# Last layer's first three groups score three quarters of the keys early; the feature bias by small products; the mixing's layernorm as a step of its own

## The chip, the cores and the metric

The kernel runs on 1 core of one Trainium2 chip. The time is the device time of one launch in microseconds (us). Five engines work side by side, each through its own queue in order: TensorE (PE in the profile; its weight loads are the row PEld), VectorE (DVE), ScalarE (ACT), GpSimd (POOL) and SyncE (SP), which here only issues DMAs.

## The reference

2048 tokens of 128 features go through four layers, each an attention and a feed-forward with a layernorm ahead of each and a residual add behind it.

```python
x = x + _L0_attn_ref(_layernorm(x), ...)   # softmax attention, 16 heads of 64
x = x + _L0_ffn_ref(_layernorm(x), ...)    # 8 experts, top one, with capacity
x = x + _L1_attn_ref(_layernorm(x), ...)   # causal attention, 16 heads of 64
x = x + _L1_ffn_ref(_layernorm(x), ...)    # mixing with the token before
x = x + _L2_attn_ref(_layernorm(x), ...)   # kernel weights that fold to one product
x = x + _L2_ffn_ref(_layernorm(x), ...)    # ternary weights, 128 -> 512 -> 128
x = x + _L3_attn_ref(_layernorm(x), ...)   # region mask and a feature bias
x = x + _L3_ffn_ref(_layernorm(x), ...)    # binary weights, 128 -> 512 -> 128
```

The parts that the change touches are the mixing and the last attention:

```python
x_prev = jnp.concatenate([jnp.zeros((B, 1, C), x.dtype), x[:, :-1, :]], axis=1)
xr = mu_r * x + (1.0 - mu_r) * x_prev
xk = mu_k * x + (1.0 - mu_k) * x_prev
r = jax.nn.sigmoid(jnp.einsum('btc,dc->btd', xr, W_r))
k_act = jnp.square(jax.nn.relu(jnp.einsum('btc,dc->btd', xk, W_k)))
out = r * jnp.einsum('btc,dc->btd', k_act, W_v)
...
hmid = jax.nn.gelu(jnp.einsum('bnd,fdk->bfnk', x, ext_w1) + ext_b1[None, :, None, :], approximate=False)
feature_scores = jax.nn.sigmoid(jnp.einsum('bfnk,fk->bfn', hmid, ext_w2) + ...).transpose(0, 2, 1)
dots = jnp.einsum('bhid,bhjd->bhij', q, k) * scale
dots = jnp.where(mask[None, None, :, :], dots, neg)
bias = jnp.einsum('bnf,hf->bhn', feature_scores, fw)[..., None]
attn = jax.nn.softmax(dots + bias, axis=-1)
```

The bias is one number for each query and head.

## The kernel before

**Tiles and stages.** The residual stream `x` lies in SBUF as 16 tiles of 128 tokens by 128 features, and its normalised transpose `xT` beside it (L277 writes it). Four tiles are a quarter of the tokens. An attention layer (class `Attention`) goes through 8 pairs of heads; a pair (class `Pair`) makes keys `kT`, queries `qT` and values `v` by quarters (L390, L399, L411, L418). Each pair has 8 groups of 256 queries (class `Group`), and a group has 8 strips of 32 queries.

**A strip.** For each of the two heads, `score` multiplies 32 queries with all keys into one PSUM bank (L482): the keys are split in four, each a product of 32 rows in its own quarter of the partitions, so a strip is a tile of 128 x 512 scores. There are four banks, two strips. `scan` (L492) lets VectorE copy a bank to SBUF (`e`) and take the minimum of each row. When four strips are scanned, `spread_lowest` brings the minima of the four parts of a query together: a transpose (L544), a reduction on VectorE (L552), a copy on GpSimd (L560), a transpose back (L567), and the shift (L586, in the last layer L578, which adds the bias; there GpSimd has first taken the bias off the minima, L536). ScalarE then makes the exponentials in place (L594), VectorE transposes them in blocks of 32 (L611), TensorE multiplies them with the values (L626), and L645 to L699 divide by the sums, project and add to `x`. The tile `e` has six buffers, two for each group in the last layer.

**The passage to the last layer.** When the second attention layer is done with a span of tokens, the function `rest` takes that span through the mixing (L1070 to L1136), the folded third attention (L1087, L1145) and the ternary feed-forward (`feed_forward`, L955 to L988), with a layernorm (`normalise`, L241 to L277) ahead of each and one more for the last layer. The spans are tiles 0 to 3, 4 to 7, 8 to 11, 12 and 13, 14 and 15. A span's mixing needs the last token of the span before; L1091 saves its column in `edge`, because the next layernorm overwrites `xT`. `features` makes the bias for a quarter: three products and Gelus (L1194, L1199), a product and a Sigmoid (L1207, L1213), then four times a GpSimd copy that repeats the scores of 32 tokens four times (L1221), four products with the weights of the heads (L1228) and a VectorE copy of 64 columns into `bias` (L1234).

**What sets the order.** No order is written by hand. Every step is a `Step` with an engine, an estimated duration, a key and the steps and buffers that it needs. The key begins with a tick, a number handed out by `planner(tick)`; smaller goes first. The function `run` goes through the steps once, keeps a clock for each engine from the estimates, and issues the first step in key order that can start, or one that fits into the time until then. What comes out is a fixed order for each engine; on the chip each engine works through its own in that order and waits for semaphores. A change of an estimate or of a tick can so move instructions anywhere. Buffers come from rings (`Ring`, `Held`), and most rings hand them out in key order. The layers' ticks are set here:

```python
L1 = Attention("L1", L0.begin + 32 * HP, 0.125 * 0.125, causal=True)
L3 = Attention("L3", L1.begin + 32 * HP, 0.125, masked=True, bias=bias)
...
for t0, n in spans:
    rest(planner(L1.left(t0, n)), t0, n, L1.outputs(t0, n) + [bu_added[t0 // 4]], n < 4, made)
```

and a group's scoring needs the keys of all four quarters:

```python
needs = pair.k_made[0 : self.g // 2 + 1 if causal else 4] + [pair.q_made[self.g // 2]]
```

Of the kernel before, what the change touches and what calls it, by code (L numbers as in the profile page):

```python
# [13 lines left out]
ALU = mybir.AluOpType  # L14
# [44 lines left out]
def network(ctx: ExitStack, tc: tile.TileContext, a: dict, out: bass.AP):  # L59
# [18 lines left out]
    class Ring:  # L78


        def __init__(self, pool, name, shape, bufs, ordered=True):
            self.bufs, self.takers, self.held, self.ordered = bufs, [], [], ordered
            self.make = lambda: pool.tile(list(shape), F32, tag=name, name=name, bufs=bufs)
            rings.append(self)

    class Held:


        def __init__(self, ring):
            self.ring, self.users = ring, []  # L90
# [28 lines left out]
    def run():  # L119
# [18 lines left out]
        for _ in range(len(steps)):  # L138
# [18 lines left out]
            for h in s.takes:  # L157
                h.t = h.ring.make()
# [30 lines left out]
    LOW, SHIFT = Ring(small, "low", [P, 2, 4], 3), Ring(small, "shift", [P, 2, 4], 3)  # L189
    ALL_LOW, ALL_LOW4 = Ring(small, "all_low", [NS, Q], 2), Ring(small, "all_low4", [NS, 4, Q], 2)  # L190
# [43 lines left out]
    def normalise(add, t0, n, after, before=(), row=None, hurry=False):  # L234


        mv, xn, pt = Held(MEANS), Held(NORMED), Held(MISC)
# [57 lines left out]
    class Attention:  # L295
# [53 lines left out]
        def plan(self):  # L349
            for p in range(HP):  # L350
# [3 lines left out]
                for g, first, weigh in groups:  # L354
                    Group(pair, g, begin + first, late, begin + weigh)
# [10 lines left out]
    class Pair:  # L366
# [19 lines left out]
        def projected(self, add, c, to, which, s, takes):  # L386
            pp, b = Held(MISC), self.layer.biases[which]
# [18 lines left out]
        def valued(self, add, c):  # L406
            pv, v = Held(MISC), self.v[c]
# [13 lines left out]
    class Group:  # L421


        def __init__(self, pair, g, t0, late, t1):
# [3 lines left out]
            self.sums, self.o, self.oT = Held(SUMS), Held(SUMMED), Held(OUT)  # L428
            self.lows, self.shifts = [Held(LOW) for j in range(2)], [Held(SHIFT) for j in range(2)]
            scanned = [self.score(planner(t0 + k, SCORES), planner(t0 + k, LOWEST), k) for k in range(4)]  # L430
# [28 lines left out]
        def score(self, add, add_scan, k):  # L459
# [5 lines left out]
            def make(i, s):  # L465
                n, strip = self.width(i), NS * self.g + i
                own = bass.ts(strip, Q)
                for h in range(2):
                    half = bass.ds(DH * h, DH)
                    for c in range(4):  # L470
                        on = bass.ts(c, Q)
                        q = pair.qT[self.g // 2].t[half, bass.ts(strip % 16, Q)]
                        keys = blocks(pair.kT.t[half, 0 : 4 * n], c)
# [3 lines left out]
                        if masked and strip == 0:  # L477
                            terms.append((0, n, picks[half, 0:Q], blocks(regions[half, :], c)))
                        if masked and c == 0:
# [10 lines left out]
            def scan(i, h, s):  # L490
                n = self.width(i)
                nc.vector.tensor_scalar(  # L492
                    self.e(h)[:, i, 0:n], s.t[:, 0:n], 1.0, None, ALU.mult, ALU.min,
                    accum_out=self.lows[j].t[:, h, i % 4 : i % 4 + 1],
                )

            needs = pair.k_made[0 : self.g // 2 + 1 if causal else 4] + [pair.q_made[self.g // 2]]
# [911 lines left out]
```

## Time and profile before

| what | value |
|---|---|
| time, median of 3 runs | 3634.2 us (3632.11 to 3635.78) |
| time of the profiled execution | 3627.2 us |
| its span, first to last instruction | 3625.3 us |
| TensorE busy, matmuls | 3522.5 us (97%) |
| VectorE busy | 3333.3 us (92%) |
| ScalarE busy | 2611.1 us (72%) |
| GpSimd busy | 574.6 us (16%) |
| L492, scans, 3072 | 1658.7 us |
| L611, transposes of the exponentials, 768 | 1504.6 us |
| L594, exponentials, 3072 | 1969.3 us |

A busy TensorE is not TensorE at its peak, since matmuls overlap and their ends are modelled; an engine that is busy in one stage can be idle in another, so the shares of the whole span say little about any stage. The page shows the span in 40 equal slices, in tenths of busy time, with the TensorE clock that was granted:

```profile
PE   8999999999999999999999988899999999999998
DVE  8999999999999979888888874699999999999995
ACT  5677777777777667788888866477776766777775
PEclk9999999999999999999999998899999999999999
```

A slice is 90.6 us. The dip of VectorE in slices 24 and 25, from about 2170 to 2350 us, is the passage to the last layer.

### The profile page before, as it was taken

To read this page: it belongs to the slowest core of one execution; us is meant where nothing else is said; L and a number is where in the kernel's file an instruction comes from. 1 tells how busy PE (TensorE), PEld (TensorE's weight loads), DVE (VectorE), ACT (ScalarE), POOL (GpSimd) and SP (SyncE) were. 2 spreads that over 40 slices of the span, in tenths; PEclk is the share of its full clock that TensorE was granted. 3 is DMA by queue.
4 is the path that set the end of the run, shared out by engine and by line. 5 is a ranking of instruction groups with operands and counts; after the bars stand their busy time and mean duration, and the time that the engine had idled before them with its cause. 6 is when DMAs were issued, how large, how long until landed. Compare 5 with 4: busy or idle time off the path is not lost. (4 is left out here: it accounts for less than half of the span.)

```text
span 3625.3 us, 112352 instructions
## 1 busy us (share of the span) xinstructions
PE 3522.5 (97%) x46250; PEld 1798.6 (50%) x46250; DVE 3333.3 (92%) x8275; ACT 2611.1 (72%) x7940; POOL 574.6 (16%) x1172
## 2 busy tenths in 40 slices
PE   8999999999999999999999988899999999999998
PEld 3444444444444455655555645445444454444544
DVE  8999999999999979888888874699999999999995
ACT  5677777777777667788888866477776766777775
POOL 1111011101111242111111134111111111111112
PEclk9999999999999999999999998899999999999999
DMA  1000000000000000000000000000000000000000
GB/s 45 2 5 2 5 5 2 5 2 5 5 2 5 1 5 8 6 6 6 6 6 6 6 2 4 4 5 5 2 5 2 5 5 2 5 2 2 2 5 10
DMA packets 22938, 18.77 MB, mean 5 GB/s; under 512 B 3556, under 2 KB 21612, under 8 KB 22426
## 3 DMA queue, kind: packets, MB, share of 16 engines
q1 hardware_dynamic: 22362, 11.55, 1.1%
q8 instruction: 363, 5.95, 0.7%
q14 instruction: 149, 1.22, 0.1%
q0 software_dynamic: 64, 0.06, 0.0%
HBM read 10.60 MB, written 1.05 MB: 3 GB/s over the span
## 5 line engine op out<-in xcount | busy, mean ns | idle before, releaser
L594 ACT ACTIVATE e<-e,shift 128x512 f32<-128x512 f32 (+15 forms) x3072 | 1969.3, 644 | 182.0 <-DVE shift L578 174.9
L492 DVE TENSOR_SCALAR_CACHE_REDUCE e<-s 128x512 f32<-128x512 f32 (+15 forms) x3072 | 1658.7, 588 | 58.1 <-PE s L482 57.0
L482 PE MATMUL s<-kT,qT 64*32 64x512 f32 (+8 forms) x24576 | 1514.0, 534 | 25.5 <-DVE e L492 24.1
L611 DVE STREAM_TRANSPOSE e<-e 128x2048 f32<-128x2048 f32 (+10 forms) x768 | 1504.6, 1961 | 21.9 <-ACT e L594 20.7
L626 PE MATMUL o<-e,v 128*64 128x256 f32 (+1 forms) x10496 | 1302.4, 386 | 13.3 <-DVE e L611 11.9
L626 PEld LDWEIGHTS o<-e,v 128*64 128x64 f32 x10496 | 731.1, 137 | 587.6 <-issue 233.4
L482 PEld LDWEIGHTS s<-kT,qT 64*32 64x32 f32 x24576 | 429.1, 105 | 490.2 <-DVE e L492 239.0
L594 ACT ACTIVATION_READ_ACCUMULATOR e<-e,shift 128x1 f32 x3072 | 580.0, 189 | 0.0
L560 POOL COPY all_low<-all_low 8x128 f32<-8x128 f32 x384 | 108.0, 281 | 1953.3 <-DVE all_low L552 1953.3
L699 POOL TENSOR_TENSOR x<-x,part 128x256 f32<-128x256 f32 x384 | 280.7, 731 | 562.8 <-ACT part L681 547.4
L681 ACT ACTIVATE part<-t,r 128x128 f32<-128x128 f32 x768 | 218.8, 366 | 148.9 <-PE t L671 144.8
L686 ACT COPY oT<-o 128x256 f32<-128x256 f32 x192 | 70.7, 368 | 274.7 <-PE o L626 274.6
L492 DVE DVE_READ_ACCUMULATOR e<-s 128x1 f32 x3072 | 229.7, 75 | 0.0
L390 PE MATMUL t<-xT,w 128*128 128x512 f32 x384 | 204.2, 625 | 2.7 <-ACT xT L277 2.0
L482 PE MATMUL s<-beyond,eye 64*32 64x32 bf16 x2560 | 159.8, 177 | 0.0
L671 PEld LDWEIGHTS t<-w,oT 64*128 64x128 f32 x1536 | 103.9, 188 | 98.3 <-issue 67.2
L671 PE MATMUL t<-w,oT 64*128 64x128 f32 x1536 | 141.4, 299 | 2.8 <-ACT oT L686 1.5
L482 PEld LDWEIGHTS <-regions 64*32 64x32 bf16 x1024 | 74.4, 93 | 130.1 <-issue 105.3
L586 ACT COPY shift<-t 128x8 f32<-128x8 f32 x256 | 42.2, 165 | 131.0 <-PE t L567 131.0
L552 DVE TENSOR_REDUCE all_low<-t 8x32 f32<-8x128 f32 x384 | 100.7, 262 | 27.8 <-PE t L544 26.9
L482 PE MATMUL s<-picks,regions 64*32 64x8 bf16 x1024 | 122.1, 166 | 0.0
L567 PEld LDWEIGHTS t<-ident,all_low 8*128 8x128 f32 x384 | 51.2, 133 | 134.9 <-issue 75.9
(181 smaller groups left out, 1790.8 us busy)
## 6 DMA issues: line engine op xcount, KB each, us to landing
w<-in_L_wq SPq DMA_DIRECT2D x24, 64.0 KB, 1.9
w<-in_L_wk SPq DMA_DIRECT2D x24, 64.0 KB, 2.1
w<-in_L_wv SPq DMA_DIRECT2D x24, 64.0 KB, 2.0
w<-in_L_wo SPq DMA_DIRECT2D x24, 64.0 KB, 2.1
x<-in_x SPq DMA_DIRECT2D x4, 256.0 KB, 4.7
out_x<-x SPq DMA_DIRECT2D x3, 256.0 KB, 2.3
big<-in_L_wo SPq DMA_DIRECT2D x1, 512.0 KB
big<-in_moe_w SPq DMA_DIRECT2D x1, 512.0 KB
```

Source lines behind the costliest of these rows:

```text
L390: nc.tensor.matmul(pp.t, lhsT=self.w.t[:, which, :], rhs=xT[:, cols(4 * c, 4)], start=True, stop=True)
L482: nc.tensor.matmul(s[h].t[on, bass.ds(first, size)], lhsT=lhsT, rhs=rhs, start=m == 0, stop=m == len(terms) - 1,)
L492: nc.vector.tensor_scalar(self.e(h)[:, i, 0:n], s.t[:, 0:n], 1.0, None, ALU.mult, ALU.min, accum_out=self.lows[j].t[:, h, i % 4 : i % 4 + 1],)
L552: lambda: nc.vector.tensor_reduce(all_low.t, pm.t[0:NS, 0:P].rearrange("p (c q) -> p q c", q=Q), AX.X, ALU.min),
L560: lambda: nc.gpsimd.tensor_copy(all_low4.t, all_low.t.unsqueeze(1).to_broadcast([NS, 4, Q])),
L594: nc.scalar.activation(e, e, AF.Exp, bias=self.shifts[j].t[:, h, i % 4 : i % 4 + 1], scale=-1.0, accum_out=self.sums.t[:, h, i : i + 1],)
L611: nc.vector.transpose(e, e)
L626: nc.tensor.matmul(self.o.t[bass.ds(DH * h, DH), first(t) : NS, :], lhsT=self.pair.v[c].t[:, t % 4, bass.ds(DH * h, DH)], rhs=self.e(h)[:, ...
L671: nc.tensor.matmul(y[h].t[:, bass.ts(j, P)], lhsT=oT.t[half, bass.ts(j, P)], rhs=pair.w.t[half, 3, :], start=True, stop=True,)
L681: nc.scalar.mul(part.t[:, j, :], y[h].t[:, bass.ts(j, P)], r.t[:, j, h : h + 1])
L686: lambda: nc.scalar.copy(oT.t, self.o.t.rearrange("p i q -> p (i q)")),
L699: POOL, 0.74, lambda part=part: nc.gpsimd.tensor_tensor(xs, xs, part.t, ALU.add), [divided], uses=[part]
```

## The change

**Early scores.** In the last layer's first pair, groups 0 to 2 score in two parts. The first part is the keys of the first three quarters (384 of the 512 columns), with a tick 12 below the layer's begin, and needs only those keys; its minima go to a ring `first_low` of six buffers. The second part is the last quarter (128 columns). A VectorE minimum (128 x 8) joins the two before the rest of `spread_lowest`. The region mask's products are split along. All other groups score as before.

**Feature bias.** GpSimd's copies are gone. The scores of a quarter, as they are, are multiplied with the weights of the heads (4 products into 64 columns), ScalarE copies these, 16 products with columns of the identity put each strip's rows into the four parts of the partitions, and one VectorE copy of 256 columns writes `bias`.

**The mixing's layernorm.** It leaves `rest` and becomes `first_norm`, which is planned for all spans ahead of the rests of all spans, with the same ticks. `edge` has a column for each tile instead of two that take turns.

**Ticks and estimates.** The last layer begins 14 ticks later. The estimates for scoring and transposing are changed. Buffers get names of their own, which changes no instruction.

```diff
+                    early = begin - 12 + first if p == 0 and g < 3 and self.masked else None
+                    Group(pair, g, begin + first, late, begin + weigh, early)
...
-            scanned = [self.score(planner(t0 + k, SCORES), planner(t0 + k, LOWEST), k) for k in range(4)]
+            parts = [(t0, 0, 4, self.lows)]
+            if early is not None:
+                self.firsts = [Held(FIRST) for j in range(2)]
+                parts = [(early, 0, 3, self.firsts), (t0, 3, 4, self.lows)]
+            scanned = [[] for k in range(4)]
+            for tick, c0, c1, lows in parts:
+                for k in range(4):
+                    scanned[k] += self.score(planner(tick + k, SCORES), planner(tick + k, LOWEST), k, c0, c1, lows)
...
-            needs = pair.k_made[0 : self.g // 2 + 1 if causal else 4] + [pair.q_made[self.g // 2]]
+            needs = pair.k_made[c0 : self.g // 2 + 1 if causal else c1] + [pair.q_made[self.g // 2]]
...
-            us = max(0.25, 0.0019 * n) + (0.1 if causal else 0.07 if masked else 0.0)
+            us = max(0.25, 0.002 * n) + (0.14 if causal else 0.05 if masked else 0.0)
...
+            for some in self.firsts[j : j + 1]:
+                found = [
+                    add(
+                        DVE,
+                        0.1,
+                        lambda some=some: nc.vector.tensor_tensor(low.t, low.t, some.t, ALU.min),
+                        found,
+                        uses=[low, some],
+                    )
+                ]
...
-            return add(DVE, 0.06 + 0.00436 * self.width(4 * j), do, made, uses=self.rows)
+            return add(DVE, 0.05 + 0.0042 * self.width(4 * j), do, made, uses=self.rows)
...
+    def first_norm(add, t0, n, after, hurry):
+        done, _ = normalise(add, t0, n, after, L1.readers[t0 // 4], hurry=hurry)
+        last = t0 + n - 1
+        to, some = edge[:, last : last + 1], xT[:, bass.ds(PAD + P * (t0 + n) - 1, 1)]
+        kept[t0 + n] = add(DVE, 0.15, lambda: nc.vector.tensor_copy(to, some), [done])
+        return done
...
+        def weigh():
+            for i in range(4):
+                nc.tensor.matmul(
+                    pbias.t[:, bass.ts(i, H)], lhsT=fs.t[0:NF, bass.ts(i, P)], rhs=fwT, start=True, stop=True
+                )
+
+        def hand_out():
+            for q in range(4):
+                for i in range(4):
+                    nc.tensor.matmul(
+                        pall.t[bass.ts(q, Q), bass.ts(i, 4 * H)],
+                        lhsT=ident[:, bass.ts(i, Q)],
+                        rhs=some.t[:, 0 : 4 * H],
+                        start=True,
+                        stop=True,
+                    )
+
+        def copy():
+            to = bias[:, bass.ts(c, 16), :].rearrange("p (t i) h -> p i t h", i=4)
+            nc.vector.tensor_copy(to, pall.t[:, 0 : 16 * H].rearrange("p (i t h) -> p i t h", i=4, h=H))
...
-            made = add(POOL, 0.6, spread, [scored], takes=[some], uses=[fs])
-            add(PE, 0.8, weigh, [made, fwT_made], takes=[pbias], uses=[some])
-            L3.biased[c].append(add(DVE, 0.16, copy, uses=[pbias]))
+        add(PE, 0.6, weigh, [scored, fwT_made], takes=[pbias, some], uses=[fs])
+        made = add(ACT, 0.25, lambda: nc.scalar.copy(some.t[:, 0 : 4 * H], pbias.t[:, 0 : 4 * H]), uses=[pbias, some])
+        add(PE, 1.2, hand_out, [made], takes=[pall], uses=[some])
+        L3.biased[c].append(add(DVE, 0.4, copy, uses=[pall]))
...
-    L3 = Attention("L3", L1.begin + 32 * HP, 0.125, masked=True, bias=bias)
+    L3 = Attention("L3", L1.begin + 32 * HP + 14, 0.125, masked=True, bias=bias)
```

## The prediction, made before the changed kernel ran

> **What bounds the kernel now.** I read the busy time by stretches of the span first, then the chain of waits through the passage from the third layer into the last one, then VectorE's and TensorE's timelines there, then the groups of instructions by shape. The windows (span 3625.3 us; columns: window, its length, busy time of each engine with its instructions, granted TensorE clock, DMA share, GB/s):
>
> ```profile
> core 0: us, PE busy (x) PEld busy (x) DVE busy (x) ACT busy (x) POOL busy (x), PEclk, DMA share, GB/s
> 2263.30:2311.90 48.60, 38.62 (x151) 28.43 (x152) 14.65 (x58) 16.52 (x37) 12.26 (x26) 0.71 0.02 6
> 2311.90:2325.00 13.10, 13.10 (x202) 5.39 (x208) 11.51 (x39) 5.20 (x9) 1.85 (x5) 1.00 0.01 3
> 2325.00:2350.00 25.00, 21.84 (x253) 10.04 (x244) 23.68 (x57) 12.53 (x37) 2.66 (x8) 0.86 0.01 1
> 2350.00:2375.00 25.00, 23.55 (x212) 12.36 (x211) 20.07 (x46) 24.36 (x50) 3.23 (x7) 0.97 0.03 11
> 2375.00:2400.00 25.00, 25.00 (x312) 12.98 (x313) 23.22 (x49) 15.24 (x45) 2.43 (x6) 0.89 0.01 2
> 2400.00:2420.00 20.00, 20.00 (x248) 9.71 (x246) 20.00 (x46) 14.08 (x41) 3.03 (x7) 1.00 0.01 2
> 2420.00:3500.00 1080.00, 1076.94 (x13493) 528.34 (x13489) 1076.15 (x2312) 767.65 (x2139) 138.52 (x340) 1.00 0.01 3
> ```
>
> From 2420 to 3500 VectorE is busy 1076.15 of 1080 us: the last layer lasts as long as its VectorE work, and whatever VectorE need not do after the last keys come ends the kernel sooner. Ahead of it lies the hole: 2263.3 (keys of the third quarter copied) to 2311.9 (keys of the last quarter copied), with VectorE busy 14.65 of 48.6 us, 33.95 us idle. What fills the hole is one chain, word for word (start, us, what):
>
> ```profile
> 2262.68 6.93 PE t L1228 x32
> 2269.61 1.15 PE t L1104 x2
> ...
> 2277.04 0.69 PE t L1104 x2
> ...
> 2280.86 0.44 DVE x L1145
> ...
> 2310.23 1.06 PE t L390 x2
> ```
>
> The first L1104 belongs to tokens 12 and 13 (in tiles of 128), the second to tiles 14 and 15; the last row makes the keys of the last quarter. And what VectorE waited for when the last layer began, and the spacing of its scans at the three widths:
>
> ```profile
> 2313.49 0.69 DVE L492 TENSOR_SCALAR_CACHE_REDUCE e<-s 128x512 f32<-128x512 f32 x1 [7.22 <-PE s L482]
> ...
> 3493.19 0.69 DVE L492 TENSOR_SCALAR_CACHE_REDUCE e<-s 128x512 f32<-128x512 f32 x1
> 3493.80 0.69 DVE L492 TENSOR_SCALAR_CACHE_REDUCE e<-s 128x512 f32<-128x512 f32 x1
> ...
> 1904.49 0.56 DVE L492 TENSOR_SCALAR_CACHE_REDUCE e<-s 128x384 f32<-128x384 f32 x1
> 1904.97 0.55 DVE L492 TENSOR_SCALAR_CACHE_REDUCE e<-s 128x384 f32<-128x384 f32 x1
> ...
> 2062.53 0.28 DVE L492 TENSOR_SCALAR_CACHE_REDUCE e<-s 128x128 f32<-128x128 f32 x1
> 2062.74 0.29 DVE L492 TENSOR_SCALAR_CACHE_REDUCE e<-s 128x128 f32<-128x128 f32 x1
> ```
>
> Start to start, accumulator read included: 0.61 us at 512 wide, 0.48 at 384, 0.21 at 128.
>
> **Early scores, what they remove.** Three groups of 8 strips by 2 heads are 48 scans. In the built program all 48 scans of 384 stand on VectorE ahead of the last quarter's keys, and 48 of 128 behind them. Behind the keys VectorE saves 48 x (0.61 - 0.21) = 19.2 us. Six combining minima of 128x8 are added there: the nearest row, L578 of the same shape, takes 0.15 us, so 6 x 0.12 = 0.7 us (0.08 to 0.15 each). Net -18.5.
>
> **What they cost in the hole.** 48 x 0.48 = 23.0 us of VectorE, under the 33.95 us idle, and 24 strips on TensorE; such a strip took 0.70 us in the third layer, so 17 us. They are hidden only if they do not hold the chain, and both queues run in order. I followed the new order step by step with the old durations.
>
> (a) Tiles 8 to 11. ScalarE now runs 8 exponentials, 4 output copies and one small copy ahead of this span's Relu, where it ran 4 exponentials: 4 x 0.71 + 1.14 + 0.25 = +4.2 us; later waits absorb a part. I take +3.5 for the keys of the third quarter.
>
> (b) Tiles 12 and 13. Between their mixing and L1145 (x += attention) VectorE's queue now holds 26 scans, 12.5 us. The old stretch from the mixing (2261.8) to L1145 (2281.3) is 19.5 us, in which VectorE worked 6.2. Most fits; scans ahead of the layernorm's scaling and of L1145 cost 2.2. L1145 comes 5.7 later.
>
> (c) Tiles 14 and 15. Their mixing used to come before the other span's L1145 (2276.4 against 2280.86); now it stands behind it, its statistics (1.2 us) and two scans (1.0). Their L1104 moves from 2277.04 to 2280.86 + 5.7 + 0.4 + 1.2 + 1.0 + 0.5 = 2289.7: +12.6.
>
> (d) From L1104 to the keys it took 34.9 us. The 20 scans left (9.6 us) lie mostly in waits for GpSimd's powers and ScalarE's copies; TensorE's steps stand behind two strips at a time. By my walk +0.2.
>
> Keys +12.8 at the old clock. Bounds: 0 (all hidden) and 36, see the slower rival. The clock: the chain's TensorE rows from 2285.6 to 2311.3 add up to 19 us in a window granted 0.71; at 1.00 they would take 13.5. With strips between them I take 2 of these 5.5 us back (0 to 5.5). **Keys +11.**
>
> [...] The rows give 0.48 + 0.21 - 0.61 = 0.08 us for a split.
>
> **Feature bias.** Gone: per quarter 4 GpSimd copies (0.60 us each), 16 matmuls and 4 VectorE copies of 64 columns (0.2 spacing). In the hole the 16 matmuls held TensorE's queue from 2262.68 to 2269.61, because GpSimd's copies fed them one at a time. New: 4 matmuls, a ScalarE copy of 64 columns (between L586's 0.165 and L686's 0.37: 0.25), 16 matmuls of 64 columns (not in the trace: 0.6, twice L645's eight in 0.31, to 4.6, four times L1087's 1.16 at the low clock; I take 2, most columns being few) and one VectorE copy of 256 (0.22 to 0.43: 0.4). This frees about 4 us of TensorE's queue, and the first strips take its place there; so it is priced in (b). Behind the keys 8 copies become 2: 8 x 0.2 - 2 x 0.4 = -0.8. The copy for the third quarter stands ahead of the first group's L552 on VectorE and waits for Sigmoid, products, copy, products: about 6.4 us after the keys; behind it wait the first shift and the exponentials, which I put 12.4 us after the keys, against 2323.65 - 2311.9 = 11.7.
>
> **First filling of the pipeline.** From 2311.9 to 2420 VectorE sat idle 108.1 - 98.5 = 9.6 us. In the new order I count 5.3 us until the first transpose (waits for strips, the copy above, the shift), then about 2: 7.5. **-2** (between -9.6 and +5).
>
> **Separate layernorm of the mixing.** The same instructions at the same priority; the edge copy no longer waits for its buffer. Its rows show no idle time before them (2261.73 follows at once), so 0, and no cover is needed.
>
> **Order elsewhere.** The new cost figures and the later start reorder the passage from the first to the second layer and the tail. TensorE was idle 310 - 290.5 = 19.5 us from 1190 to 1500, the most that could be won; a loss of the same size is the other bound. I take 0, and 5 either way in the range. No DMA is added.
>
> **Sum.** -18.5 - 0.8 + 11 - 2 = -10.3. Profiled execution: span 3625.3 to 3615.0, its time 3627.2 to 3616.9. The median of the runs, 3634.2, lies 7.0 above that execution; the same difference gives **3624**.
>
> **Rivals.**
> - Hidden fully: the keys come only 3.5 later (step a). For it: 33.95 us idle against 23.0. Against: (c) is an order that no slack mends. -18.5 - 0.8 - 2 + 3.5 = -17.8: 3616.
> - Cancelled: nearly every scan holds the chain, keys +20. For it: in-order queues, and a chain of some 40 short steps. -1.3: 3633.
> - Slower: TensorE's chain steps stand behind strips, the strips behind banks, the banks behind scans that stand behind the chain's own VectorE step, so the fill adds in full: 23.0 + 3.5 + 10 such meetings x 0.97 (two scans) = keys +36. For it: the built order shows ten. Against: only 4 banks, so a meeting costs what is left of two strips. -21.3 + 36 = +14.7: 3649. It decides from keys +28.6.
> - The order elsewhere loses over 10 us and hides the gain: 3636.
>
> **Chances.** A measurement of this kernel tells 0.2%, 7.3 us, from no change: under 3626.9 is faster, over 3641.5 slower. Forecast 0.40, hidden fully 0.17 (both faster, mostly: 0.56), cancelled or lost elsewhere 0.27, slower 0.16 (0.17 with the tail of the others). The range 3611 to 3644 holds 8 in 10.
>
> **What would show it.** The last quarter's keys near 2322; the hole's VectorE busy share up from 0.30 to 0.7 and its clock above 0.71; 96 scans of 384 and 128 in place of 48; VectorE full again within 15 us of the keys; the stretch from the keys to the end about 21 us shorter. Wrong if the keys come before 2316 or after 2330, or if the passage before 1500 moves by over 5 us.

## The result: slower, and the profile after

The changed kernel took 3636.7 us (median of 22 runs, 3632.6 to 3651.9) against 3631.1 us for the kernel before (22 runs, 3626.2 to 3635.8). The ratio is 1.0022, 95% interval 1.0015 to 1.0030: slower by about 0.2%, where 0.28% faster was forecast.

The profiled execution was one of the long ones: its span is 3647.4 us. An execution of the same kernel at 3634.7 us was profiled in the first experiment (e1, span 3632.6), so both are shown. The table gives the start of some copies of the last layer's or second layer's keys to SBUF (ScalarE, L399 before, L401 after), and how much later they start in each profile than before. The columns of experiments are used further below.

| milestone | before, us | after | e1 | e2 | e9 | e14 | e18 |
|---|---|---|---|---|---|---|---|
| keys inside the second layer | 1512.5 | +12.4 | +5.1 | -0.9 | +3.7 | +5.5 | +1.8 |
| last keys of the second layer | 2022.6 | +21.0 | +7.9 | -1.1 | +2.9 | +4.7 | +1.2 |
| last layer, third quarter's keys | 2262.7 | +23.3 | +8.5 | +3.2 | +0.2 | +5.5 | -1.4 |
| last layer, last quarter's keys | 2311.3 | +35.6 | +20.9 | +13.3 | +10.3 | -2.6 | -11.5 |
| first keys after VectorE is full | 2571.7 | +19.6 | +4.8 | -6.6 | -9.5 | -7.1 | -17.2 |
| end of the span | 3625.3 | +22.1 | +7.3 | -4.6 | -7.4 | -3.3 | -12.6 |

Read down a column: what is lost or won between two milestones is the difference of two rows. Already at the end of the second layer, far ahead of the early scores, the changed kernel is 21.0 us late in one profile and 7.9 in the other. From there to the last quarter's keys it loses another 14.6 (13.0 in e1), behind the keys it wins 16.0 (16.1), and in the rest of the last layer it loses 2.5 again in both profiles. From the keys to the end it is so 13.5 us shorter, where 21 were forecast.

The windows of the changed kernel's profile, in the columns used before: the hole from the third to the last quarter's keys, the 20 us behind it, the rest of the filling, and the last layer.

```profile
2286.60:2347.57 60.97, 52.27 (x584) 29.29 (x580) 37.37 (x151) 16.66 (x36) 11.35 (x24) 0.91 0.02 6
2347.57:2367.57 20.00, 19.96 (x385) 11.91 (x392) 11.20 (x84) 12.95 (x22) 1.66 (x7) 0.91 0.06 17
2367.57:2420.00 52.43, 43.66 (x581) 21.65 (x565) 50.67 (x118) 40.41 (x115) 4.42 (x13) 0.90 0.01 2
2420.00:3500.00 1080.00, 1079.72 (x13534) 531.77 (x13531) 1073.75 (x2290) 764.57 (x2135) 134.70 (x334) 1.00 0.01 3
```

VectorE (third pair of numbers) now works 37.37 of 60.97 us in the hole, 0.61 against 0.30 before, and the granted clock there rose from 0.71 to 0.91. The hole itself grew from 48.6 to 61.0 us. In the first 20 us behind the keys VectorE works only 11.20; before it worked 18.06 in such a window. The last layer is still VectorE's.

The chain of waits through the hole, the rows that answer to those shown of before (start, us, what):

```profile
2290.90 0.66 PE pk L1127 x2
2291.55 1.47 PE s L493 x18
...
2307.32 0.43 DVE x L1167
...
2309.70 1.52 PE s L493 x8
2311.25 1.22 PE pk L1127 x2
...
2345.87 1.05 PE pp L392 x2
```

The order is the one that the prediction walked through: the mixing of tiles 14 and 15 (the second pk) stands behind x += attention of tiles 12 and 13 (L1167), and strips (s) stand between.

### The profile page after: what moved, and what is told of

Its sections match the earlier page's. It is cut to its first block, busy times and chain, and to the rows that moved or that the text cites. A ratio compares the mean times of both kernels' runs of the same rounds, so it can differ in the third digit from the quotient of the medians.

```text
span 3647.4 us, 113232 instructions
## 1 busy us (share of the span) xinstructions
PE 3535.8 (97%) x46674; PEld 1797.3 (49%) x46674; DVE 3335.9 (91%) x8365; ACT 2612.8 (72%) x7943; POOL 565.4 (16%) x1156
## 5 line engine op out<-in xcount | busy, mean ns | idle before, releaser
L493 PE MATMUL s<-kT,qT 64*32 64x512 f32 (+12 forms) x24960 | 1523.2, 529 | 38.5 <-DVE e L503 37.5
L647 PE MATMUL o<-e,v 128*64 128x256 f32 (+1 forms) x10496 | 1306.7, 387 | 9.2 <-DVE e L632 8.9
L647 PEld LDWEIGHTS o<-e,v 128*64 128x64 f32 x10496 | 727.8, 138 | 601.7 <-issue 248.2
L702 ACT ACTIVATE part<-y,r 128x128 f32<-128x128 f32 x768 | 218.4, 367 | 146.4 <-PE y L692 139.2
L392 PE MATMUL pp<-xT,w 128*128 128x512 f32 x384 | 208.9, 635 | 3.7 <-ACT part L702 3.0
L692 PEld LDWEIGHTS y<-w,oT 64*128 64x128 f32 x1536 | 106.5, 187 | 91.6 <-issue 62.2
L692 PE MATMUL y<-w,oT 64*128 64x128 f32 x1536 | 143.5, 299 | 1.5 <-ACT oT L707 0.8
L607 ACT COPY shift<-pm 128x8 f32<-128x8 f32 x256 | 42.2, 165 | 131.1 <-PE pm L588 131.1
L588 PEld LDWEIGHTS pm<-ident,all_low 8*128 8x128 f32 x384 | 51.2, 133 | 147.5 <-issue 87.9
L493 PEld LDWEIGHTS <-eye 64*32 64x32 bf16 x2560 | 98.9, 95 | 38.4 <-issue 16.6
```

Source lines behind the costliest of these rows:

```text
L392: nc.tensor.matmul(pp.t, lhsT=self.w.t[:, which, :], rhs=xT[:, cols(4 * c, 4)], start=True, stop=True)
L493: nc.tensor.matmul(s[h].t[on, bass.ds(first, size)], lhsT=lhsT, rhs=rhs, start=m == 0, stop=m == len(terms) - 1,)
L588: lambda: nc.tensor.transpose(pm2.t[:, 0:NS], all_low4.t.rearrange("p c q -> p (c q)"), ident[0:NS, 0:NS]),
L647: nc.tensor.matmul(self.o.t[bass.ds(DH * h, DH), first(t) : NS, :], lhsT=self.pair.v[c].t[:, t % 4, bass.ds(DH * h, DH)], rhs=self.e(h)[:, ...
L692: nc.tensor.matmul(y[h].t[:, bass.ts(j, P)], lhsT=oT.t[half, bass.ts(j, P)], rhs=pair.w.t[half, 3, :], start=True, stop=True,)
L702: nc.scalar.mul(part.t[:, j, :], y[h].t[:, bass.ts(j, P)], r.t[:, j, h : h + 1])
```

## The experiments

Each was timed in up to five rounds beside the kernel before on the same chip; e4 and e14 have 6 executions, e18 has 5, the others 11 or 12. "Parts" names what of the change each kernel has: E early scores, B new feature bias, S the last layer's later start, s the new cost figure of the scores, t that of the transposes, D the last quarter's features held back (not part of the change). The layernorm's split is left out of the letters: the changed kernel and its variants have it, the ones made from the kernel before do not.

| run | parts | median, us | before, us | ratio | 95% interval |
|---|---|---|---|---|---|
| changed | E B S s t | 3636.7 | 3631.1 | 1.0022 | 1.0015 to 1.0030 |
| e1 | E B S s t | 3639.6 | 3630.1 | 1.0029 | 1.0018 to 1.0039 |
| e2 | E B S | 3627.0 | 3630.1 | 0.9997 | 0.9988 to 1.0006 |
| e3 | s t | 3635.2 | 3630.1 | 1.0013 | 1.0004 to 1.0022 |
| e4 | E S | 3643.4 | 3630.1 | 1.0035 | 1.0023 to 1.0047 |
| e5 | B | 3632.0 | 3631.1 | 0.9998 | 0.9989 to 1.0006 |
| e6 | B S | 3625.6 | 3631.1 | 0.9982 | 0.9974 to 0.9991 |
| e7 | E B S D | 3627.6 | 3631.1 | 0.9984 | 0.9975 to 0.9992 |
| e8 | s | 3634.3 | 3631.1 | 1.0007 | 0.9999 to 1.0016 |
| e9 | E B S s | 3620.0 | 3631.3 | 0.9973 | 0.9964 to 0.9982 |
| e10 | E B S, s and t in the last layer | 3631.8 | 3631.3 | 1.0003 | 0.9994 to 1.0012 |
| e11 | B S D | 3625.4 | 3631.3 | 0.9987 | 0.9978 to 0.9996 |
| e12 | as e11, E for one group | 3628.6 | 3631.3 | 0.9995 | 0.9986 to 1.0004 |
| e13 | E B S s D | 3622.6 | 3632.2 | 0.9970 | 0.9960 to 0.9980 |
| e14 | B S s | 3619.0 | 3632.2 | 0.9968 | 0.9956 to 0.9980 |
| e15 | E B S s, t in the last layer | 3626.5 | 3632.2 | 0.9986 | 0.9978 to 0.9995 |
| e16 | E B S s, t in the first two | 3634.3 | 3632.2 | 1.0013 | 1.0005 to 1.0022 |
| e17 | S | 3640.6 | 3630.9 | 1.0022 | 1.0013 to 1.0031 |
| e18 | B S s D | 3614.6 | 3630.9 | 0.9957 | 0.9945 to 0.9970 |

A difference of 0.0001 is 0.36 us. Where two kernels of different rounds are compared, the difference of their ratios is used; it is known to 0.0012 to 0.0016.

### e1: the changed kernel again

No edit.

> The changed kernel once more, for a second profile beside the first (span 3647.4 us, the passage to the second layer 12 us later than before, the second layer another 9 us longer at a granted clock of 0.98, the passage to the last layer about even). Theory A (the second layer's loss is a clock drop that only some executions take, since one idle stretch of TensorE in each head pair sits at its edge): an execution near 3634 us shows the second layer at a clock of 1.00 and no more than 3 us longer than before, and its time comes out 0.1 to 0.3% above before. Rival B (the loss of the second layer is work or waiting that every execution has): it is 9 us longer again.

Measured: 1.0029, and a profile that is 2.9 us longer than before through the second layer (5.1 to 7.9 in the table) where the first profile is 8.6 longer, at clock 1.00 against drops to 0.91 over 20 us. The two profiles part by 14.8 us, and 13.1 of that is there by the end of the second layer. Theory A: the clock drop is taken by some executions. That an idle stretch of TensorE sits at the edge of a drop, no run shows. Of the 13.1, 7.3 are there at the keys of 1512.5; ahead of them the first profile has the clock at half for 13.65 us on end (second window below), where e1 has it for 6.83 at most; why is not known. The other 5.8 fall in the second layer, and there the place shows in the rows. In the second layer the changed kernel has the products of weights and values (L647) behind the narrow strips of 32 keys; TensorE's timeline of the first profile, and behind it four windows: the 10 us around these rows, the 13.65 us named above, and the 3.4 us ahead of the drop and of the drop itself (the granted clock is the third number from the right):

```profile
1562.36 0.27 PE L493 MATMUL s<-kT,qT 64*32 64x32 f32 x7 [0.32 <-DVE e L503]
...
1562.97 0.29 PE L493 MATMUL s<-kT,qT 64*32 64x32 f32 x8 [0.32 <-DVE e L503]
...
1563.58 0.34 PE L493 MATMUL s<-kT,qT 64*32 64x32 f32 x8 [0.29 <-DVE e L503]
...
1563.88 3.23 PE L647 MATMUL o<-e,v 128*64 128x256 f32 x16
```

```profile
1560.00:1570.00 10.00, 8.96 (x154) 5.17 (x147) 8.91 (x31) 7.09 (x24) 1.98 (x4) 0.83 0.01 2
1354.88:1368.53 13.65, 12.96 (x69) 5.81 (x68) 5.71 (x21) 5.79 (x20) 1.93 (x4) 0.50 0.00 0
1559.70:1563.10 3.40, 2.66 (x82) 1.49 (x68) 3.40 (x11) 3.25 (x13) 1.70 (x3) 1.00 0.03 7
1563.10:1566.50 3.40, 3.11 (x36) 1.77 (x34) 3.23 (x13) 3.40 (x11) 0.00 (x0) 0.50 0.00 0
```

The strips are thin and wait for banks (0.3 us each, for VectorE's scans); the 16 products behind them then take 3.23 us. In e1's profile they take 1.95 in the same place of the same order:

```profile
1556.46 1.95 PE L647 MATMUL o<-e,v 128*64 128x256 f32 x16
1559.01 1.95 PE L647 MATMUL o<-e,v 128*64 128x256 f32 x16
```

The kernel before has them ahead of the strips, and TensorE is busy 9.88 of 10 us there:

```profile
1548.55 1.95 PE L626 MATMUL o<-e,v 128*64 128x256 f32 x16
1550.43 0.28 PE L482 MATMUL s<-kT,qT 64*32 64x32 f32 x12
```

The pattern comes once in each pair of heads. From the keys of one pair to those of the next it is 102.0 us before, 102.6 in e1, e3 and e16, which have it, and 101.9 in e8 and e9, which do not; in the first profile it is 104.0 in the four of five pairs where the clock dropped and 102.6 in the fifth. The second layer is TensorE's (505.62 of 513.10 us busy in e1, VectorE 451.75), so its pauses count: ahead of the narrow strips it sits idle 5.3 us in e1 from the keys of 1512.5 to the last ones, and 0.6 before.

### e2, e3, e4: the cost figures and the early scores apart

e2 takes the cost figures back; e3 does only this, in the kernel before, the other way round:

```diff
-            us = max(0.25, 0.002 * n) + (0.14 if causal else 0.05 if masked else 0.0)
+            us = max(0.25, 0.0019 * n) + (0.1 if causal else 0.07 if masked else 0.0)
...
-            return add(DVE, 0.05 + 0.0042 * self.width(4 * j), do, made, uses=self.rows)
+            return add(DVE, 0.06 + 0.00436 * self.width(4 * j), do, made, uses=self.rows)
```

e4 puts the early scores and the later start alone into the kernel before:

```diff
+                    early = begin - 12 + first if p == 0 and g < 3 and self.masked else None
...
-    L3 = Attention("L3", L1.begin + 32 * HP, 0.125, masked=True, bias=bias)
+    L3 = Attention("L3", L1.begin + 32 * HP + 14, 0.125, masked=True, bias=bias)
```

> The changed kernel with the three old cost figures of the planner; up to the passage into the last layer its instructions then stand in the order of the kernel before. Theory A (the new cost figures lose the time, in the first and second layer; early scores, bias path and layernorm are about even): at the time of before, within 3 us, with the second layer's first keys at 1242 and the last quarter's keys of the last layer at 2322 to 2328 us. Rival C (the early scores hold the chain and lose the time themselves): still 4 us or more above before. Rival D (the early scores do win what was forecast and the cost figures ate it): 7 to 10 us under before.

> The kernel before with the three new cost figures alone. Theory A: 4 to 7 us above before (up to 20 in an execution that takes the clock drop), with the first keys of the second layer some 12 us later than before. Rival C: within 2 us of before, the loss lying in the early scores.

> The kernel before with the early scores and the last layer's later start alone: old cost figures, old feature bias, old layernorm. If the early scores alone are worth what the sum of the prediction gave without the bias path: 5 to 9 us under before. If the keys come some 16 us later and the stretch behind them is only 14 us shorter, as in the changed kernel's profile: within 3 us of before. If the new bias path is what makes the first exponentials late (four table loads between the keys and them), this kernel has them within 13 us of the keys, against 15.9 in the changed kernel and 12.3 before, and is 3 us better than the changed kernel with the old cost figures.

Measured: e2 0.9997, e3 1.0013, e4 1.0035. The cost figures lose about 5 us by themselves and 9 to 12 in the changed kernel (1.0022 and 1.0029 against 0.9997). Rival C falls for e2, and so does D. But e4 missed its expectation by far: with the old bias path the early scores and the later start cost 13 us, its keys come 22.4 us later than before (27.9, less 5.5 at the end of the second layer), and its first exponential 19.8 us behind them. So the parts do not add.

### e5, e6, e7, e8: one part at a time

e5 is the new `features` in the kernel before. e6 is e2 with `g < 0` for `g < 3`, so that no group scores early. e8 is the kernel before with the new figure of the scores alone. e7 is e2 with the last quarter's features behind the first group's exponentials:

```diff
-        features(planner((L1.left(8, 4) - 1, L1.left(12, 2) - 1, L1.left(14, 2) + 1, L1.left(14, 2) + 2)[c]), c)
+        features(planner((L1.left(8, 4) - 1, L1.left(12, 2) - 1, L1.left(14, 2) + 1, L3.begin + 8)[c]), c)
...
+        last_features = steps[seen:]
     L3.plan()
+    for s in last_features:
+        s.after.append(L3.exped[3])
```

(`exped` collects the layer's steps of exponentials.)

> The kernel before with the new feature bias alone. The early scores alone (old bias path) cost 13 us (1.0035), with the new bias path and the layernorm, at the old cost figures, the kernel is level with the one before (0.9997). Theory A (the bias path is worth something only together with the early scores, since in the early kernel GpSimd's copies feed TensorE's queue one product at a time in front of the strips): 0 to 5 us under before. Rival B (the bias path is worth its 10 to 15 us by itself and the early scores cost as much): 8 us or more under before.

> The changed kernel with the old cost figures and without the early scores (bias path, layernorm and the last layer's later start stay). If the early scores win anything: slower than the same kernel with them (3627 median) by 1 to 6 us, the last quarter's keys 8 to 15 us earlier than with them (2324.7) and the stretch behind the keys 14 to 20 us longer. If they lose: 3622 or less.

> The changed kernel with the old cost figures, the last quarter's features held back until the first group's exponentials. Theory A (the pipeline behind the keys fills late because the features of the last two quarters stand in front of the first exponentials on ScalarE and of the strips on TensorE: shift at 12.5 us behind the keys, table loaded until 14.3, first transpose at 19.2): first exponentials within 11 us of the keys, first transpose within 15, the kernel 3 to 5 us faster than with the features in front (3627), 5 to 8 under before. Rival B (the wait for the features is taken up later, VectorE has other work): within 1 us of 3627.

> The kernel before with the new cost figure of the scores alone, not that of the transposes. In its built order the product of weights and values stands ahead of the narrow strips in the second layer, as before; with both figures it stands behind them. Theory A (that swap makes the idle stretch at which the clock drops): the second layer as long as before within 1 us in its profile, no execution with a mean clock under 0.982, and within 3 us of before. Rival B (the loss comes from the reordered passage between the first two layers): 4 to 6 us above before, as with both figures.

e5: 0.9998, theory A: by itself the bias path is worth nothing. e6: 0.9982; the kernel without the early scores is, if anything, faster than with them. e8: 1.0007; its second layer is as long as before (from -2.0 to -2.7 in the milestones), but it is not quite level.

e7: 0.9984 against 0.9997, with intervals that overlap. ScalarE's timelines behind the last quarter's keys, first the changed kernel's:

```profile
2346.97 0.60 ACT L401 ACTIVATE kT<-pp 128x512 f32<-128x512 f32 x1 [3.45 <-PE pp L392]
2347.58 1.28 ACT L1255 ACT_TABLE_LOAD   x1
...
2349.57 1.28 ACT L1220 ACT_TABLE_LOAD   x1
...
2357.15 0.68 ACT L1220 ACTIVATE hm<-ph,ext_b 64x512 f32<-64x512 f32 x1 [2.90 <-PE ph L1215]
2357.84 1.28 ACT L1255 ACT_TABLE_LOAD   x1
2360.85 0.68 ACT L1255 ACTIVATE fs<-pf,ext_b 5x512 f32<-5x512 f32 x1 [1.72 <-PE pf L1228]
2361.55 1.28 ACT L615 ACT_TABLE_LOAD   x1
2362.84 0.72 ACT L615 ACTIVATE e<-e,shift 128x512 f32<-128x512 f32 x1
```

Four table loads of 1.28 us and the whole feature network of the last quarter stand between the keys and the first exponential, 15.9 us behind them (14.3 in e2). On VectorE the first transpose is 20.7 us behind; what it waits for between its first strip behind the keys and then, the longest three:

```profile
2354.11 0.29 DVE L503 TENSOR_SCALAR_CACHE_REDUCE e<-s 128x128 f32<-128x128 f32 x1 [3.00 <-PE s L493]
2356.08 0.42 DVE L1251 COPY bias<-pall 128x256 f32<-128x256 f32 x1 [0.84 <-PE pall L1241]
...
2361.01 0.17 DVE L599 TENSOR_TENSOR shift<-pm,bias 128x8 f32<-128x8 f32 x1 [2.21 <-PE pm L588]
```

Strips and the spreading of the minima stand on TensorE behind the feature products, whose rows in the changed kernel's chain add up to 9.08 of the 13.88 us from 2346.93 to 2360.81; TensorE's products have no idle time before them there, and its weight loads wait 0.4 us for ScalarE. ScalarE in e7:

```profile
2333.81 0.60 ACT L401 ACTIVATE kT<-pp 128x512 f32<-128x512 f32 x1 [3.44 <-PE pp L392]
2334.42 1.28 ACT L1256 ACT_TABLE_LOAD   x1
...
2338.68 1.28 ACT L616 ACT_TABLE_LOAD   x1
2341.11 0.72 ACT L616 ACTIVATE e<-e,shift 128x512 f32<-128x512 f32 x1 [1.15 <-DVE shift L600]
```

Two loads, the exponential 7.3 us behind the keys, the first transpose 10.2. VectorE's idle time in the 100 us behind the keys, from the timelines: 9.6 us before, 10.6 in the changed kernel, 8.7 in e2, 5.2 in e7.

### e9 to e12: one figure back, and fewer early scores

e9 takes back one line of the change, the figure of the transposes:

```diff
-            return add(DVE, 0.05 + 0.0042 * self.width(4 * j), do, made, uses=self.rows)
+            return add(DVE, 0.06 + 0.00436 * self.width(4 * j), do, made, uses=self.rows)
```

e10 has both new figures only where `masked` (the last layer). e11 and e12 are e7 with `g < 0` and `g < 1`.

> The changed kernel with the old cost figure of the transposes; the scores keep their new one. In the second layer the product of weights and values then stands ahead of the narrow strips again, as in the kernel before; the rest of the change stays. Theory A (the swap of these two, which takes both figures, is what makes the second layer longer and lets the clock drop): second layer within 1 us of before in its profile, no execution over 3643 us or under a mean clock of 0.982, median 3 to 8 us under the changed kernel (3637 to 3640). Rival B (the loss is the reordered passage between the first two layers or the last layer's own order): still 5 us or more above before, with executions near 3650.

> The changed kernel with the new cost figures in the last layer alone: the first two layers stand in the order of before. Theory A (the loss lies in the first two layers): as with the old figures everywhere, 3624 to 3630 (0.9997). Rival B (the last layer's own order loses it: VectorE 10.5 us idle behind the keys against 8.7, half a microsecond lost at most of the later passages between heads, a longer end): 3 us or more above that, 3630 to 3635.

> The changed kernel with the old cost figures, without the early scores, the last quarter's features held back until the first group's exponentials. Theory A (the early scores cost about as much ahead of the keys as they save behind them): level with the early kernel so deferred (0.9984), within 0.0008. Rival B (the early scores lose 5 us, as the pair 0.9997 and 0.9982 suggests, and the deferring wins as much without them): 0.9970 or less. Rival C (deferring without early scores wins nothing, since VectorE is busy with scans of 512 while ScalarE works on the features): 0.9982.

> The same with one early group (16 scans) in place of three (48). If each early scan costs its share of the 17.5 us by which the keys of the early kernel are later than without it: keys 6 us later than without early scores and 12 earlier than with three. If only the scans ahead of the mixing of tokens 12 to 15 cost, and the last groups lie in real idle time: keys 10 us or more later than without. Time: between the kernels with none and with three, unless the first group's scans are the free ones; then faster than both, 0.997.

e9: 0.9973, 10 us faster than before and 18 to 20 us faster than the changed kernel, more than was expected. In its profile the second layer is 0.8 us shorter than before (3.7 to 2.9), its products stand ahead of the strips, and its last quarter's keys are 7.4 us late against the end of the second layer, not 13 to 14.6:

```profile
2263.50:2322.25 58.75, 50.04 (x575) 26.54 (x569) 37.75 (x151) 16.59 (x36) 11.40 (x24) 0.94 0.02 6
2322.25:2342.25 20.00, 18.88 (x401) 11.50 (x400) 12.73 (x85) 14.49 (x26) 1.68 (x7) 1.00 0.05 16
```

The hole is as full as the changed kernel's (37.75 us of VectorE) and 2.2 us shorter. e10: 1.0003, with a median in the range of rival B; it is 4.7 us over e2 by medians, 2.2 by ratios, and the intervals overlap: the last layer's own order under the new figures may lose some of it, not all. e11: 0.9987, level with e7 (theory A). e12 is no better than either, so the first group's scans are not free ones; its keys are 1.1 us late against the end of the second layer (+6.0 less 4.9), where e11's are 3.3 early and e7's 16.6 late. One group so costs 4.4 us of the 19.9 that three cost, less than a third.

### e13 to e16: where the figure's 18 us go

e13 is e9 with the deferred features, e14 is e9 without early scores; e15 and e16 split the new figure of the transposes by layer (e15's edit; in e16 the two formulas change places):

```diff
-            return add(DVE, 0.05 + 0.0042 * self.width(4 * j), do, made, uses=self.rows)
+            return add(DVE, (0.05 + 0.0042 * self.width(4 * j) if self.layer.masked else 0.06 + 0.00436 * self.width(4 * j)), do, made, uses=self.rows)
```

> The changed kernel with the old figure of the transposes, and the last quarter's features held back until the first group's exponentials. Deferring was worth 1 to 5 us with all figures old (0.9997 to 0.9984; VectorE's idle time behind the keys 8.7 to 5.2 us). If the two gains add: 0.9960 to 0.9970, median 3615 to 3619. If the deferring only shifts the wait: 0.9973.

> The changed kernel with the old figure of the transposes and without the early scores. Theory A (early scores are about even: 17 us later keys against 15 to 20 us saved behind them): within 2 us of the same kernel with them (3620). Theory B (in this order, where the mixing of tokens 8 to 15 starts 7 us earlier against the end of the second layer, the early scores do win): 4 us or more slower than with them. Theory C (they lose here as with the old figures, 0.9982 against 0.9997): 4 us or more faster, 3616 or less.

> The changed kernel with the new figure of the transposes in the last layer alone, the old one in the first two. The new figure cost 18 us in all (1.0022 to 1.0029 against 0.9973). From the profiles: 9 us of it in the last layer and the passage into it (keys 2.3 later, 3.7 less won behind them, 0.6 later on, 2.3 in the mixing of tokens 8 to 11), so 3626 to 3630 here. Rival (it all lies in the first two layers): 3620.

> The changed kernel with the new figure of the transposes in the first two layers alone. From the profiles the swap in the second layer costs 3.6 us in every execution and 9 to 12 where the clock drops, with 1.4 in the passage before it: 3625 to 3632, and some executions above 3636 with a mean clock under 0.984. Rival (it all lies in the last layer): 3620 and no such executions.

Against e9, e15 is 4.7 us slower (0.9986) and e16 14.5 (1.0013), by the medians 6.5 and 14.3; together 19.2, the whole of the figure's loss, though the 4.7 alone is hardly clear of noise. In e16's profile the second layer adds 2.9 us (4.8 to 7.7), 3.7 more than in e9; the rest of its 14.2 us over e9's span is spread over the passage ahead of that (1.1), the passage to the last layer (5.5), the filling (1.3) and the last layer with its end (2.7), and no row there is as plain as the strips'. It had one execution of 11 over 3640 us; the changed kernel had 7 of 22 and 5 of 11, e9 none of 11.

e14: 0.9968, theory A: the early scores are about even. e13: 0.9970: the deferring, 5 us in e7, adds next to nothing here.

### e17, e18: the later start, and the fastest form

e17 is the kernel before with the `+ 14` alone; e18 is e14 with e7's deferring.

> The kernel before with the last layer's later start (14 ticks) alone. With the new bias path the later start went from 0.9998 to 0.9982; the separate layernorm moves no instruction of note there. Theory A (the later start wins 6 us by itself): 0.9980 to 0.9985. Rival B (it wins only with the new bias path): within 0.0008 of 1.

> The changed kernel with the old figure of the transposes, without the early scores and with the last quarter's features held back: the candidate for the fastest. With early scores the deferring moved 0.9973 to 0.9970, without them and with all figures old 0.9982 to 0.9987. If deferring is worth nothing: 0.9968 as without it; if it wins its 2 to 3 us: 0.9960.

e17: 1.0022, 8 us slower. Both theories failed: the later start wins 6 us with the new bias path (e5 to e6; e6 also has the layernorm's split) and loses 8 without it. In its profile the first exponential comes 23.8 us behind the keys and the first transpose 31.8. e18: 0.9957, the fastest found, 16 us under before, though its interval overlaps those of e13 and e14. Over the four pairs that differ by the deferring alone (e2 and e7, e6 and e11, e9 and e13, e14 and e18) the ratio moves by -0.0013, +0.0005, -0.0003 and -0.0011: about 2 us won, if any. e18's windows:

```profile
2261.90:2300.45 38.55, 28.52 (x142) 18.56 (x138) 14.04 (x55) 16.29 (x37) 11.04 (x24) 0.87 0.02 8
2300.45:2320.45 20.00, 19.67 (x287) 8.89 (x290) 17.12 (x50) 10.63 (x23) 0.97 (x4) 1.00 0.01 2
```

Its hole is 38.55 us, 10 shorter than before, with as little of VectorE's work in it: 14.04 us against 14.65.

## Why the prediction was wrong, step by step

**What bounds the kernel** was right: behind 2420 us VectorE is busy 1073.75 of 1080 us. That holds for the last layer; the second is TensorE's, as shown at e1.

**The sum, term by term**, in e1's profile, whose clock did not drop in the second layer: order up to the end of the second layer +7.9 (forecast 0), the keys against that +13.0 (forecast 11), the stretch behind the keys -16.1 (forecast -21.3), the rest of the last layer +2.5 (forecast 0); together +7.3 where -10.3 was forecast. The forecast's time also lies 3 us high for another reason: it was reckoned from a median of 3 runs, 3634.2, and that of 22 is 3631.1. Both of its signs of being wrong came up: keys after 2330, and the passage before 1500 moved by more than 5 us.

**Order elsewhere, "I take 0, and 5 either way in the range"** is the step that failed. By the end of the second layer the changed kernel is 7.9 us late, or 21.0 when the clock drops, and its last layer loses 2.5 more behind the filling. With one cost figure, that of the transposes, set back (e9), the sign of the result turns: 0.9973, a gain of 9.8 us against the 10.3 forecast. The figure costs 18 to 20 us, about 14.5 by the first two layers and 4.7 by the last. One place is shown by rows, the products of weights and values behind the narrow strips (3.7 us between e16 and e9, more when the clock drops); how the rest divides over single swaps was not settled. A rival of the prediction, order elsewhere that loses over 10 us, named 3636; the time was 3636.7.

**The agreement of e9 with the forecast is partly chance.** There the new figure of the scores makes the stretch from the second layer's last keys to the third quarter's 7 us shorter than in e2 (from +2.9 to +0.2 against -1.1 to +3.2), which the prediction had not foreseen, and the early scores give less than it said. In all that figure wins 9 us there (e2 to e9), and alone in the kernel before it wins nothing (e8, 1.0007); in which layer it wins was not tried.

**Early scores, behind the keys: forecast 21.3 us with the bias copies and the filling, measured 16.0 (16.1 in e1), and 19.9 in e2 and 19.8 in e9.** Of the 5.3 missing in the changed kernel 3.1 are the filling: VectorE's idle time went from 9.6 to 10.6 us where 7.5 was forecast. The prediction had the copy of the third quarter's bias in front of the shift, but not that the last quarter's feature network would stand there too. With the old figure of the transposes (e9) 3.8 of the 5.3 come back, 1.9 of them in the filling (8.7 us idle).

**Early scores, ahead of the keys: steps (a) to (c) were right.** Against the end of the second layer (21.0), the third quarter's keys are 2.3 us late (3.5 forecast), L1167 5.5 (5.7) and the mixing of tiles 14 and 15 13.2 (12.6). The strips of 384 keys whose time the forecast took stand in the second layer; the third has none.

**(d) and the clock.** From that mixing to the keys 1.4 us were lost where 0.2 was lost and 2 won back in the forecast; the 2 was the author's choice between 0 and 5.5, and no run shows it. The clock of the hole's last 26 us did rise, from 0.76 (2285.6 to 2311.9) to 0.94 (2321.0 to 2347.6), but the mean of a window did not tell what a row in it would gain. The last feed-forward's two products took 3.41 + 2.43 = 5.84 us before, 2.64 + 2.79 = 5.43 after and 3.94 in e2; the features' last product (L1207 before, L1228 after) took 2.76 in all three. The clock granted over just these rows fits that, the feed-forward before, after and in e2, then the features' product before:

```profile
2297.25:2303.09 5.84, 5.84 (x26) 5.12 (x25) 0.00 (x0) 2.26 (x5) 0.10 (x1) 0.60 0.00 0
2333.31:2338.74 5.43, 5.43 (x25) 5.01 (x26) 0.00 (x0) 1.85 (x4) 0.00 (x0) 0.69 0.01 3
2312.51:2316.45 3.94, 3.94 (x25) 3.54 (x26) 0.00 (x0) 1.77 (x4) 0.00 (x0) 1.00 0.02 4
2307.47:2310.23 2.76, 2.76 (x8) 0.35 (x7) 0.00 (x0) 0.41 (x2) 0.31 (x1) 1.00 0.00 0
```

In the changed kernel one stretch at half the clock (2334.51 to 2337.92, granted 0.50) lies on the feed-forward's products, and the features' product had the full clock already before.

**The whole of the early scores is about even.** Five pairs of kernels differ by them alone (e17 and e4, e6 and e2, e14 and e9, e11 and e7, e18 and e13): +0.0013, +0.0015, +0.0005, -0.0003, +0.0013, a mean of +0.0009 or 3 us lost, each pair known to 0.0012 to 0.0016 only. In the profiles of e14 and e9 they bring the keys 14.7 us later (-7.3 to +7.4 against the second layer's end) and save 15.3 behind them. The forecast charged 11 and saved 18.5. It measured both against the hole of the kernel before, while the rest of the change, with the old figure of the transposes, brings the keys sooner by itself (e14: by 7.3 us), which the early scores then give up.

**Feature bias.** By itself 0.9998, as small as forecast. What was not forecast is that it decides what the later start does (e17 1.0022, e6 0.9982). **Layernorm: 0** fits: in the program, taking its split back moves one instruction, a copy of one column on VectorE, by 15 places and leaves every other in its order. Such a kernel was not run.

## What to carry to other kernels

Where a planner orders the instructions, a cost figure is a change with a price of its own: build each figure and each part alone before crediting the part with a name, since here one line cost more than all the others won. How near a figure is to the chip did not tell which order is better: from the start of a transpose of 2048 columns to that of VectorE's next instruction it is 2.23 us (median, the kernel before and the changed one), where the old figure said 2.29 and the new one 2.20, so the new one is nearer there, and yet e15, which has it in the last layer, where nearly all are of 2048, was not the faster; at 1024 columns it is 1.16, and the old figure, 1.176, is nearer than the new one, 1.125. Filling VectorE's idle time in front of a chain delayed the chain here (keys 14.7 us later, e14 to e9), and what it saves behind has to be more than that; with 15.3 us saved it was about even, and e18, whose keys come 12.7 us sooner against the end of the second layer, was the fastest.

## What the runs showed of the hardware

TensorE's clock dropped in a stretch where it was never idle for long: with pauses of 0.3 us between strips of 0.3 us, and 8.96 us busy of 10, the clock was 0.83 and 16 products took 3.23 us instead of 1.95, in one execution of a program and not in another (1.00 and 1.95, 8.94 busy of 10). The longest executions of the changed kernel, e1 and e16, which have that order, lie 15.3, 12.5 and 9.8 us above their medians; in e3, which has it too, it is 6.2, and in the kernels without it 1.3 to 8.2. In the changed kernel the seven executions over 3640 us have a mean clock of 0.980 to 0.984, the others 0.983 to 0.986. So the tail fits the drop, but of that order four executions were profiled, and one of them shows it.

No long pause stands ahead of that drop: in the 3.40 us ahead of it TensorE was busy 2.66, with pauses of at most 0.32 us between its strips, at a clock of 1.00, and in the next 3.40 us it was busy 3.11 at 0.50 (third and fourth windows at e1). The same program meets the drop in one execution and not in another, as the two profiles show; what makes the clock fall, no run here shows.

Executions of one order also differ in the passage to the second layer: ten profiles whose instructions stand as in the kernel before up to there (before, e2, e4 to e7, e10 to e12, e17) have the keys of 1512.5 us shifted by -3.1, -0.9, 0 and, in seven of them, by 4.7 to 5.9. A single profile can't tell less than that from a change; here that took the medians.
